# A four-layer network on one core: layer 0's attention as one chain over four quarters, layer 2's attention by rows as they are gathered

## The chip, the cores and the metric

The kernel runs on one core of one Trainium2 chip. The metric is the device time of one execution in microseconds (us), the median over several runs. A core has five engines that work side by side, each through its own queue in order: PE (TensorE, matrix products and transposes), DVE (VectorE), ACT (ScalarE), POOL (GpSimd) and SP (SyncE, which here only starts DMAs). POOL also starts the indirect DMAs, which gather or scatter single rows by a list of indices.

## The reference

Four layers of attention and feed-forward, with a layer norm behind each half, on x of 4 batches x 1024 tokens x 128 features, all float32:

```python
x = L0_attn_x
x = _layernorm(x + _L0_attn_ref(x, ...))   # convolution of 4 taps, cos/sin features, cumsum over time
x = _layernorm(x + _L0_ffn_ref(x, ...))    # x and weight rounded to an fp6 grid in blocks of 32, one product
x = _layernorm(x + _L1_attn_ref(x, ...))   # linear recurrence over time with a complex diagonal
x = _layernorm(x + _L1_ffn_ref(x, ...))    # 16 experts, the best 4 of each token, and a shared one
x = _layernorm(x + _L2_attn_ref(x, ...))   # causal softmax attention, 16 heads of 8 features, rotary
x = _layernorm(x + _L2_ffn_ref(x, ...))    # 8 experts, the best 2 of each token
x = _layernorm(x + _L3_attn_ref(x, ...))   # gated Toeplitz mixing
x = _layernorm(x + _L3_ffn_ref(x, ...))    # 32 experts, the best 4 of each token, and a shared one
return x
```

Layer 0's attention and layer 1's recurrence run along time, so a later part of the sequence needs the state of the earlier one, and layer 2 is causal. A router decides per token which experts it goes to.

## The kernel before

**Tiles.** The 4 x 1024 tokens are 32 tiles of 128. A quarter is 256 time steps of all four batches, 8 tiles; a half is two quarters. `tile_of` says which tile holds which piece of a batch. `x` holds the tokens with a token per partition, `xT` the same with a feature per partition.

**Generators.** Every stage is a Python generator that emits instructions and yields what they are thought to cost, a number in the manner of us. `run` emits one to its end. `mix(main, side)` emits a step of `main` and then as much of `side` as makes up its cost, times `pace`; each instruction of the side is put behind the latest of the main one on its engine (`queued`). With `drain=False` the rest of the side is left for later. `chain` puts generators one behind the other, `abreast` emits several in step, `press` emits a side until a condition holds. The order inside an engine's queue is then made from this order and from what each instruction waits for, so instructions without such a tie can stand earlier than they were emitted.

**Experts.** A router (`l1_route`) finds each token's experts and the position of each of its rows in a list that is sorted by expert (`positions`). `spread` scatters the tokens' rows into that list in DRAM, one indirect DMA of 128 rows for each tile and choice (64 for a half in layer 1). `small_experts` loads the list in groups of 512 rows, applies the experts' weights and stores the results; `collect` gathers them back, again 128 rows a DMA, and adds them, weighted, on DVE (L1359).

**The order before, up to layer 2.** Layer 0's attention of quarters 0 and 1 (`l0_attn((0, 1))`) with nothing beside it. The set-ups of layers 1 and 2. Layer 0's FFN and layer 1's recurrence of these two quarters, the latter beside the building of layer 2's expert weights (`l2_weights`). The first half's router. Layer 0's attention of quarters 2 and 3, its products on DVE instead of POOL (`no_pool`), beside the 64 scatters of the first half. The first half's experts, beside FFN and recurrence of quarters 2 and 3 (`beside=True`: in the side's PSUM). The shared expert with what is left of that side, beside `l1_close`, which collects the first half by quarters, normalizes and transposes it. Layer 2's attention of the first half, beside router and scatters of the second half. The second half's experts, layer 2's experts of the first half, layer 2's attention of the second half (`l2_attn(1)`) beside layer 2's results and layer 3's attention of the first half, and so on to the end of layer 3.

**PSUM.** The pool `side` has two buffers of one bank with the tag "s". Layer 0's attention holds one of them for `ms` through a whole quarter, from its first product (`headd` with `den`) to the square root `rs`, and takes the other for `z2` and `po`. The recurrence (`l1_attn`) keeps two, `pu[0]` and `pu[1]`, at the same time, since both are read for the real and for the imaginary part.

**Names.** In `l0_attn`: `t`, `k` (L432-L435) the phase and its rounding, `im`, `re` (L437, L440) sine and cosine, `times` (L442) their product with `pq`, `s` the cumulative sum (L358). In `l0_ffn`: `qt`, `xd` the rounding (four passes on POOL a quarter: L485, L495, L497, L525). In `l1_attn`: `b` (L641), `g` (L645). `norm` has three ways to the inverse root: ACT's square root, POOL's power, and Newton steps on DVE (`by="dve"`); its last step is L205. In `l2_attn`: `project` and `masks` make `qT` and `qm`, `scores` the products `sc` on PE, `weights` the exponential `pr` on ACT (L1049) and the mask multiplication on DVE (L1055), `values_of` the product with the values on PE (L157).

## Time and profile before

| What | us |
|---|---|
| Median of 11 runs (2535.01 to 2555.37) | 2545.76 |
| The profiled execution | 2543.54 |
| Its span, first to last instruction | 2541.6 |
| PE busy in it | 1697.8 (67%) |
| DVE busy | 1348.7 (53%) |
| ACT busy | 811.3 (32%) |
| POOL busy | 782.6 (31%) |
| First scatter of the first half (`l1ra`) starts | 311.87 |
| First rows of the experts' list load (`xg`) | 432.02 |
| First projection of layer 2's first half | 655.06 |
| PE clock granted, mean | 0.823 of full speed |

The profile gives, for one execution, the busy time of each engine (per stretch of time, if asked), the groups of instructions by line of the program with their mean durations and with what ended the engine's waits before them, and the chain that ended last: from the last instruction back, at each step to what released it. "Another core or an unknown queue" in that chain is a wait whose end the profile can't put down to an instruction; "issue" is time in which the engine waited for nothing that the profile shows. An operation is written as output<-inputs, by the program's names.

### The profile page before, as it was taken

How to read it: one execution, taken by the hardware profiler on the slowest of the kernel's cores; microseconds unless marked ns; L12 is line 12 of the kernel's file. 1: busy time of each engine (PE TensorE's matmuls, PEld its weight loads, DVE VectorE, ACT ScalarE, POOL GpSimd, SP SyncE). 2: the span in 40 equal slices, each digit the busy share in tenths (PEclk: the TensorE clock that was granted, in tenths of full speed). 3: DMA queues.
4: the chain of work that ended last, by engine and by line, in shares of the span. 5: the costliest groups of instructions: out<-in, count | busy, mean ns of one | idle time of the engine just before them, and what ended most of it. 6: DMA issues, size and time to landing. Idle time of an engine off the chain costs nothing.

```text
span 2541.6 us, 28615 instructions
## 1 busy us (share of the span) xinstructions
PE 1697.8 (67%) x9605; PEld 1030.7 (41%) x9605; DVE 1348.7 (53%) x3797; ACT 811.3 (32%) x1158; POOL 782.6 (31%) x725
## 2 busy tenths in 40 slices
PE   7538676873651875788897888868619896764810
PEld 3225333752320454555532332345416683642710
DVE  8864795856560672234546674735403565630453
ACT  5512362320320442222365545512102352320310
POOL 5432185235145004233220001020560203154364
PEclk9768787986775997898899988978859997876865
DMA  9902002341001143222300000030410331321422
GB/s 318 289 15 87 15 35 101 105 132 43 20 27 40 52 147 103 77 63 58 111 22 1 1 5 13 14 125 25 176 56 17 106 106 43 92 84 53 117 77 53
DMA packets 224007, 192.05 MB, mean 76 GB/s; under 512 B 16816, under 2 KB 204080, under 8 KB 222832
## 3 DMA queue, kind: packets, MB, share of 16 engines
q1 hardware_dynamic: 203152, 147.28, 18.4%
q0 software_dynamic: 20704, 42.86, 5.5%
q8 instruction: 83, 1.36, 0.2%
q14 instruction: 68, 0.56, 0.1%
HBM read 93.47 MB, written 96.60 MB: 75 GB/s over the span
## 4 chain that ended last, share of the span: by engine, by line
PE 41%; DVE 21%; another core or an unknown queue 14%; POOL 9%; issue 8%; ACT 3%; DMA 3%; SPq 0%; DVEq 0%; POOLq 0%; ACTq 0%
PE gu L157 11%; PE s L157 10%; PE sc L157 5%; PE yp L157 5%; PE tp L165 5%; POOL l1ra L1293 4%; POOL yt L1293 2%; DVE x L1359 1%; PE pu L157 1%; DVE pr L1055 1%; PE pg L157 1%; POOL l3rb L1293 1%; PE py L157 1%; DVE x L205 1%
## 5 line engine op out<-in xcount | busy, mean ns | idle before, releaser
L1049 ACT ACTIVATE pr<-sc 128x1024 f32<-128x1024 f32 x288 | 279.6, 1021 | 318.2 <-PE sc L157 217.5
L157 PE MATMUL gu<-ld,xgT 128*128 x768 | 204.1, 409 | 55.0 <-ACT xgT L167 21.5
L157 PE MATMUL sc<-qm,kT 32*128 32x512 f32 (+3 forms) x1536 | 199.4, 558 | 9.8 <-ACT pr L1049 6.2
L157 PE MATMUL s<-pr,va 128*32 128x512 f32 (+3 forms) x1536 | 178.0, 533 | 41.7 <-issue 23.8
L157 PE MATMUL gu<-wall,xgT 128*128 x352 | 182.4, 645 | 20.0 <-DMA wall<-wall 18.0
L157 PEld LDWEIGHTS gu<-ld,xgT 128*128 128x128 f32 x768 | 146.2, 201 | 86.8 <-ACT xgT L167 32.8
L165 PE MATMUL tp<-ld,hg 128*128 128x128 f32 x736 | 119.2, 284 | 92.0 <-ACT hT L167 38.3
L169 DVE COPY hT<-tp 128x512 f32<-128x512 f32 x140 | 95.7, 684 | 130.3 <-PE tp L165 71.9
L165 PEld LDWEIGHTS tp<-ld,hg 128*128 128x128 f32 x736 | 94.9, 147 | 151.5 <-issue 55.9
L1462 ACT ACTIVATE sg<-gu 128x512 f32<-128x512 f32 x88 | 52.4, 598 | 289.3 <-PE gu L157 182.2
L1689 DVE TENSOR_TENSOR hg<-sg,gu 128x256 f32<-128x256 f32 x192 | 78.4, 415 | 124.8 <-ACT sg L1688 112.4
L1055 DVE TENSOR_TENSOR pr<-pr,ld 128x512 f32<-128x512 f32 (+1 forms) x160 | 92.3, 580 | 96.9 <-ACT pr L1049 88.1
L157 PEld LDWEIGHTS sc<-qm,kT 32*128 32x128 f32 x1536 | 85.3, 197 | 114.9 <-issue 71.4
L1688 ACT ACTIVATE sg<-gu 128x256 f32<-128x256 f32 x192 | 73.0, 385 | 167.4 <-PE gu L157 109.7
L1464 DVE TENSOR_TENSOR hg<-sg,gu 128x512 f32<-128x512 f32 x88 | 60.0, 681 | 121.2 <-ACT sg L1462 78.2
L165 PE MATMUL tp<-ld,xg 128*128 128x128 f32 x472 | 78.3, 291 | 64.9 <-ACT hT L167 20.5
L167 ACT COPY xgT<-tp 128x512 f32<-128x512 f32 x118 | 69.2, 586 | 159.0 <-PE tp L165 130.0
L1293 POOL DMA_INDIRECT l1ra<-x,posl1a x64 | 95.6, 1494 | 60.7 <-DVE posl1a L1270 41.5
L1293 POOL DMA_INDIRECT yt<-l1yr,posl1r x64 | 60.8, 950 | 151.5 <-DVE x L1359 76.5
L157 PE MATMUL yp<-ld,hT 128*128 x768 | 103.9, 277 | 0.7 <-DVE hT L169 0.3
L157 PEld LDWEIGHTS s<-pr,va 128*32 128x32 f32 x1536 | 38.5, 113 | 151.9 <-issue 105.6
L157 PE MATMUL yp<-wall,hT 128*128 x704 | 98.5, 286 | 1.5 <-DVE hT L169 1.5
(433 smaller groups left out, 3527.7 us busy)
## 6 DMA issues: line engine op xcount, KB each, us to landing
wall<-wall SPq DMA_DIRECT2D x16, 768.0 KB
l3ra<-zero SPq DMA_DIRECT2D x1, 6144.0 KB
wall<-we SPq DMA_DIRECT2D x24, 256.0 KB
ld<-in_l_w SPq DMA_DIRECT2D x2, 3072.0 KB
ld<-in_l_w SPq DMA_DIRECT2D x1, 6144.0 KB
xg<-l3ra SPq DMA_DIRECT2D x24, 256.0 KB
l3ya<-yg SPq DMA_DIRECT2D x24, 256.0 KB
l1ra<-zero SPq DMA_DIRECT2D x1, 5120.0 KB
```

What stands on the lines that cost most here:

```text
L157: return self.nc.tensor.matmul(out, lhsT, rhs, start=start, stop=stop)
L165: nc.tensor.transpose(pt[:, k * P : (k + 1) * P], s, self.ident)
L167: nc.scalar.copy(dst, pt[:, : n * P])
L169: nc.vector.tensor_copy(dst, pt[:, : n * P])
L205: nc.vector.tensor_scalar(x, x, mv[:, t, 0:1], rstd[:, t : t + 1], ALU.subtract, ALU.mult)
L1049: nc.scalar.activation(pr, sc[h], AF.Exp)
L1055: nc.vector.tensor_tensor(d, d, cst["tril"].unsqueeze(1).unsqueeze(1).to_broadcast([P, 2, n, P]), ALU.mult)
L1293: ins = self.nc.gpsimd.indirect_dma_start(**kw)
L1462: nc.scalar.activation(sg, gu[:, 0, :], AF.Silu)
L1464: nc.vector.tensor_tensor(h, sg, gu[:, 1, :], ALU.mult)
L1688: nc.scalar.activation(sg, pg[:, :, 0, :], AF.Silu)
L1689: nc.vector.tensor_tensor(h[:, 2 * c : 2 * c + 2, :], sg, pg[:, :, 1, :], ALU.mult)
```

## The change

Layer 0's attention is one generator over all four quarters, the main one of one `mix`. Its side is, for each quarter as soon as its attention is listed (`after`), the FFN and the recurrence, and between quarters 1 and 2 the first half's router, then scatters and layer 2's weights abreast. The side is emitted with `pace=0.45`, and what is left of it goes on beside the shared expert and the experts of the first half, which now come in this order. `l1_close` goes by batches instead of quarters and is the side of layer 2's first half, together with the second half's router and scatters; `l2_attn` presses its side until a batch's row is listed before it prepares that batch, and counts its steps as 3.8 (first half) or 3.0 (second) instead of 2.3. The second half's `l1_wall` is loaded behind layer 2's first half. `norm` can do its last step on ACT (`on_act`). Some buffers change: `den`, `b` and `g` one each, `t` and `k` three, `im` and `re` in their place.

```diff
@@ Kernel.__init__
-        self.both = (self.first, Part("r", 2, 2))
+        self.both = (Part("a", 0, 2, range(B)), Part("r", 2, 2, range(B)))
@@ norm
+        if on_act:
+            off = self.tile(self.small, [P, n], f"off{n}")
+            nc.vector.scalar_tensor_tensor(off, mv[:, :, 0], -1.0, rstd, ALU.mult, ALU.mult)
         for t, x in enumerate(tiles):
-            nc.vector.tensor_scalar(x, x, mv[:, t, 0:1], rstd[:, t : t + 1], ALU.subtract, ALU.mult)
+            if on_act:
+                nc.scalar.activation(x, x, AF.Identity, bias=off[:, t : t + 1], scale=rstd[:, t : t + 1])
+            else:
+                nc.vector.tensor_scalar(x, x, mv[:, t, 0:1], rstd[:, t : t + 1], ALU.subtract, ALU.mult)
@@ l0_attn
-        times = nc.vector.tensor_tensor if no_pool else nc.gpsimd.tensor_tensor
+        times = lambda q: nc.vector.tensor_tensor if q in no_pool else nc.gpsimd.tensor_tensor
...
-                den = self.tile(bp, [P, QC], "den")
+                den = self.tile(bp, [P, QC], "den", bufs=1)
...
-                    t = self.tile(tp, [P, QC], "t")
+                    t = self.tile(tp, [P, QC], "t", bufs=3)
...
-                    k = self.tile(tp, [P, QC], "k")
+                    k = self.tile(tp, [P, QC], "k", bufs=3)
...
-                    im = self.tile(tp, [P, QC], "im")
+                    im, re = t, k
...
-                self.norm(self.quarter(q), by="act" if no_pool else "pool")
+                self.norm(self.quarter(q), by="act" if q in no_pool else "pool", on_act=True)
+                self.listed.add(f"l0 {q}")
@@ l0_ffn
-            qp = self.pool(ctx, "l0fq", 2, right=beside)
-            ps = self.side if beside else self.pool(ctx, "l0fps", 2, space=PSUM)
+            qp = self.pool(ctx, f"l0fq{qs[0]}", 1, right=True)
+            ps = self.side
...
-                self.norm(self.quarter(q), by="dve" if beside else "act")
+                self.norm(self.quarter(q), by="dve", on_act=True)
@@ l1_attn
-            tp = self.pool(ctx, "l1t", 2, right=beside)
-            ps = self.side if beside else self.pool(ctx, "l1ps", 2, space=PSUM)
+            tp = self.pool(ctx, f"l1t{qs[0]}", 1, right=True)
+            ps = self.side
...
-                (tt if beside else nc.gpsimd.tensor_tensor)(rows(g[0]), rows(g[0]), steps(pw[:, 0, :]), ALU.mult)
+                tt(rows(g[0]), rows(g[0]), steps(pw[:, 0, :]), ALU.mult)
...
-                self.norm(self.quarter(q), by="dve" if beside else "act")
+                self.norm(self.quarter(q), by="dve", on_act=True)
@@ l1_close
-        for q in range(part.q0, part.q0 + part.nq):
-            yield from self.collect("l1", part, K1, yp, (q - part.q0) * QT, QT)
-            self.norm(self.quarter(q))
...
+        for b in range(B):
+            yield from self.collect("l1", part, K1, yp, b * 4, 4)
+            tiles = part.order[b * 4 : b * 4 + 4]
+            self.norm([x[:, t, :] for t in tiles], by="dve")
+            for t in tiles[::2]:
+                nc.sync.dma_start(out=self.xsave[:, t : t + 2, :], in_=x[:, t : t + 2, :])
...
+            nc.vector.tensor_copy(xTv[:, b, 2 * hf : 2 * hf + 2, :], pt.rearrange("p (q t) -> p q t", q=2))
+            self.listed.add(f"row {hf}{b}")
@@ l2_attn, prepare(b)
+                self.press(side, lambda: f"row {hf}{b}" in self.listed)
@@ l2_attn, main loop
-                    took += 2.3
+                    took += 3.0 if hf else 3.8
@@ l2_weights
-                    nc.gpsimd.tensor_scalar(am, ab[:, i, :], self.cst["em"][:, e : e + 1], 2.0, ALU.mult, ALU.mult)
+                    nc.scalar.activation(am, ab[:, i, :], AF.Copy, scale=em[:, e : e + 1])
@@ new
+    def after(self, q):
+        yield from self.when(lambda: f"l0 {q}" in self.listed)
+        if q == 0:
+            self.l1_setup()
+            yield (20.0,)
+            self.l2_setup()
+            self.zero_lists("l1")
+            yield (4.0,)
@@ all
-                self.run(self.l0_attn((0, 1)))
-                self.l1_setup()
-                self.l2_setup()
-                weights = self.l2_weights()
-                next(weights)
-                self.zero_lists("l1")
-                self.run(self.l0_ffn((0, 1)))
-                self.run(self.mix(self.l1_attn((0, 1)), weights))
-
-                self.run(self.l1_route(a))
-                self.run(self.mix(self.l0_attn((2, 3), True), self.spread("l1", a, K1)))
+                main = self.l0_attn(range(NQT), (2, 3))
+                then = lambda q: self.chain(self.after(q), self.l0_ffn((q,)), self.l1_attn((q,)))
+                side = self.chain(
+                    then(0), then(1), self.l1_route(a1), self.abreast(self.spread("l1", a1, K1), self.l2_weights()),
+                    then(2), then(3),
+                )
+                self.run(self.mix(main, side, pace=0.45, drain=False))
                 self.zero_lists("l2", "l3")
                 with ExitStack() as c2:
                     wall = self.l1_wall(c2)
-                    yp = self.pool(c2, "l1ya", 5, right=True)
-                    side = self.chain(self.l0_ffn((2, 3), True), self.l1_attn((2, 3), True))
-                    self.run(self.mix(self.l1_experts(a, wall), side, drain=False))
-                    self.run(self.mix(self.chain(self.l1_shared(a), side), self.l1_close(a, yp)))
+                    self.press(side, lambda: "l1a" in self.listed)
+                    self.run(self.mix(self.chain(self.l1_shared(a1), self.l1_experts(a1, wall)), side))
+            with ExitStack() as c2:
+                yp = self.pool(c2, "l1ya", 5, right=True)
+                side = self.abreast(self.l1_close(a1, yp), self.chain(self.l1_route(r), self.spread("l1", r, K1)))
+                self.run(self.mix(self.l2_attn(0, side), side))
             with ExitStack() as c2:
                 wall = self.l1_wall(c2)
-                self.run(self.mix(self.l2_attn(0), self.chain(self.l1_route(r), self.spread("l1", r, K1))))
                 wall2 = self.l2_wall(c2)
...
-            self.run(self.mix(self.l2_attn(1), on, drain=False))
+            self.run(self.mix(self.l2_attn(1, on), on, drain=False))
```

## The prediction

> **What bounds the kernel now.** I read the stretches between the program's stages first (busy time of each engine), then the chain that ended last, then the timelines of the software DMA (POOL's gathers and scatters) and of PE beside them.
>
> Stretches (us, PE, PE load, DVE, ACT, POOL busy with instruction counts, PE clock, DMA share, GB/s): the first half's layers 0 and 1 up to its router; the second half's layer 0 attention beside the first half's scatter; the first half's experts; the rest up to layer 2; layer 2's first half.
>
> ```profile
> 154.00:310.00 156.00, 99.46 (x382) 60.59 (x386) 89.88 (x287) 35.20 (x54) 36.79 (x34) 0.77 0.11 41
> 310.00:432.00 122.00, 79.73 (x364) 37.36 (x356) 102.73 (x161) 61.52 (x70) 95.62 (x64) 0.79 0.16 61
> 432.00:540.00 108.00, 91.91 (x580) 78.63 (x580) 84.03 (x211) 38.36 (x79) 18.97 (x8) 0.96 0.34 98
> 540.00:660.00 120.00, 47.44 (x171) 29.34 (x172) 61.26 (x215) 12.54 (x20) 66.12 (x64) 0.63 0.26 81
> 655.00:927.00 272.00, 168.40 (x1297) 81.51 (x1295) 135.44 (x427) 86.18 (x91) 61.67 (x64) 0.78 0.09 35
> ```
>
> Two stretches have no busy engine. From 154 to 310 DVE works 58% of the time, and layer 0's other two quarters, which are mostly DVE work, wait behind it. From 540 to 660 PE works 47 of 120 us: POOL fetches the first half's 64 result rows, and layer 2 starts only when both quarters are collected. In 310 to 432 DVE is at 84%, and the 64 scatters last as long as the attention.
>
> The chain that ended last has 14% of the span under "another core or an unknown queue". Its largest piece lies in layer 2's first half; the lines after it are the stretches of that stall, of two runs of gathers in layer 2's second half, and of a clean piece of layer 2.
>
> ```profile
> 743.41 11.54 another core or an unknown queue
> 756.00 61.97 another core or an unknown queue
> ```
> ```profile
> 740.30:820.40 80.10, 13.46 (x56) 5.41 (x48) 4.84 (x13) 4.10 (x4) 52.27 (x55) 0.52 0.11 45
> 820.00:900.00 80.00, 69.55 (x587) 32.67 (x591) 51.23 (x133) 36.22 (x38) 0.00 (x0) 0.89 0.10 42
> 1261.20:1283.70 22.50, 17.67 (x98) 4.95 (x93) 6.10 (x11) 11.26 (x12) 8.27 (x9) 0.85 0.12 29
> 1312.00:1332.00 20.00, 18.61 (x152) 6.68 (x150) 10.82 (x40) 14.22 (x15) 6.66 (x6) 1.00 0.15 44
> ```
>
> While 64 scatters run back to back PE completes 56 matmuls in 80 us, against 587 in the next 80: about 75 us lost, 1.17 us a scatter. Twenty gathers beside layer 2 left 98 matmuls in 22.5 us where 164 would fit (9 us lost, 0.45 us each); twelve looser ones cost nothing. The first half's scatter shows no such stall. The cause isn't in the trace; I use the prices.
>
> **The sum** is made against the profiled execution, 2543.54 us (span 2541.6 and 1.9 outside); the median of the runs is 2.2 above it, which I add at the end.
>
> *1. The chain over four quarters, up to the first half's experts.* Before, scatters start at 311.87 and the first expert rows load at 432.0. After, the scatters need layer 0's FFN and layer 1's scan of quarters 0 and 1 and the router. The code decides how early: the side pool has two PSUM buffers; `ms` holds one for a whole main quarter, and `l1_attn` needs two at once (both `pu` are read for r = 0 and 1). So a quarter's scan can pass only between one `ms` and the next, and I expect the second scan when quarter 2 ends. DVE work up to then: 11 us idle at the start, 27 of setups (0-154 has 122 busy; two quarters take about 48 each), two POOL-helped quarters 96, one without POOL 53 (102.7 and some 8 ahead of 310, for two), two FFNs 33 (154-205 has 33.1), two scans 36 (205-285 has 35.9), part of quarter 3 18, three quarters of the router 15 (20.9 in 285-310): 289 us. DVE was 88% busy in 318-424 and 99.6% in 322-400; at 0.93, between the two, 11 + 278 / 0.93 gives 310, the start it has now (289 to 327 at the ends). So this edit brings **0** at this point; what it brings is that both attention quarters, and part of quarter 2's FFN, are behind us there. From there 64 scatters at 1.8 us (311.87 to 426.7) as now, or 1.265 if DVE leaves POOL alone. Bounds: start at 270 and 1.265 each, experts at 385 (-47); or see the third rival.
>
> The norm's last step goes to ACT: eight DVE instructions, 2.14 us a norm, for eight on ACT of about 0.28 (between 0.19 for 128x4 and 0.385 for 128x256, an estimate), 12 norms, 27 us on an engine 40% busy: hidden, and DVE's 26 us pay for the two Newton norms a quarter (some 2.5 us) and for L663 moved from POOL (1.2 instead of 3.3). `am` on ACT: 24 x 0.28, off POOL, where it would stand behind the scatters. `zero_lists` issues the same DMAs on SP, whose queue was full from 20 to 135 and idle to 220: nothing. One buffer less for `den`, `b` and `g` and the in-place `im`, `re`: nothing while the quarter's other tiles have three.
>
> The Trainium skill speaks against laying this scatter beside still more DVE work: "SBUF — State Buffer", section "SBUF: two separate sides", says that POOL's DMA descriptors can't be written while DVE holds the shared port in a two-port mode. This case's rows agree in direction: the 64 scatters beside the attention mean 1494 ns, the second half's gathers 950. By the lock alone, taken for every scatter, they would last longer than their 115 us; by the trace (DVE already 88% busy beside them in 318-424) they stay there, and I go by the trace.
>
> *2. From the experts to layer 2's first query.* Before 432 to 655: 223 us. After: `l1_shared` (542-583 with its waits, 22 clean) goes ahead of the experts, under the scatters' tail. Experts: 20 groups of 3.54 us (1002-1037) are 71 bare; beside FFN and scan of two quarters they took 108 (432-540). Some of quarter 2's side is done, but its four POOL passes (9.5 us a quarter) stand behind the scatters in POOL's queue, so I take 95. Then only batch 0's rows: 16 gathers of 1.25, 3 us landing, 16 adds of 0.34 partly under them, a norm, turn and copy of 7: 33 with PE idle. 128: **-95**. Bounds: 71 + 28 (-124) and 108 + 20 of a late scan + 33 (-62). The second half's router (20.9 of DVE) runs inside the 33, where DVE is free.
>
> *3. Layer 2's first half.* Before 272 us, 75 of them the stall. The same 64 scatters stay; 48 gathers (batches 1 to 3) come beside them, alternating on POOL. Bounds: 0 (the loose gathers) and 1.17 each, 56 us. The nearest row is that of gathers beside layer 2, 0.45: 22. On DVE 48 adds of 0.34, three norms, four copies stand in order ahead of the mask multiplications (L1055), which PE's value matmuls wait for; an add whose gather is late stops both. DVE is half busy: 8. **+30**, up to 60. `xsave` becomes 8 DMAs of 0.33 on SP: nothing.
>
> *4. The expert weights.* `l1_wall` moves behind layer 2's first half: 3 MB that were loaded under it now stand ahead of the second half's experts, on SP ahead of `l2_wall`'s eight. The nearest row is the wait for weights at 1659.81, 13.97 us; traffic reaches 2.75 MB in 10 us. **+12** (0 if memory is free early, 14).
>
> *5. Layer 2's second half* takes its side at 3.0 a step instead of 2.3, so layer 3's attention of the first half moves some 70 steps' cost from behind 1650 to before it, where PE is 82% busy. It can close part of the gap ahead of layer 3's scatter (1765-1790, PE 17 of 25), and lengthens 1248-1650. **0** (-15 to +12). The closing by rows in the second half has the same 64 gathers: nothing.
>
> Sum: 0 - 95 + 30 + 12 + 0 = -53: 2490.5, plus 2.2 for the median, 2492.7; as term 1's near bound (a start at 289 instead of 310) only lowers it, I say **2490**.
>
> **Rivals.** (a) *The side leads.* The scan of quarter 1 finds both PSUM buffers while quarter 2's `ms` isn't taken yet; scatters start near 270. For it: the pace of 0.45 puts the side early in program order. Against: `ms` of the next quarter is ready at once, the scan only after an FFN of 30 us. -53 - 45: 2446.
> (b) *POOL starves layer 2.* All 112 DMAs run dense, 1.17 each, and gathers wait behind scatters: 56 + 12 of DVE waits instead of 30: 2530. For it: a batch's 16 gathers and up to 26 scatters take 53 us, its attention 42. Against: no stall in the two looser rows.
> (c) *Slower: the side is shut out.* If no scan passes before the main chain ends, the chain takes DVE's 244 us (11 + 27 + 96 + 110) at 0.84, 290 us; then 156 us for FFN, scan and router as in 154-310, then 81 + 7 of scatters: experts at 534 instead of 432. 2493 + 102: 2595. It decides once experts start after 485. For it: the two buffers; PE's queue is in order, so a `pu` waiting for a buffer holds the main matmuls behind it. Against: at each quarter's end `ms` is free.
> (d) *The change does not do what it says:* layer 2 still waits for all rows. For it: `press` asks only at emission. Then 48 more gathers of 1.25 stand before it, 60 us instead of the 30 beside it: about 2520, inside the range.
>
> **How the numbers follow.** Forecast (with d) 0.46, its own range 2455 to 2525; (a) 0.18, 2400 to 2455; (b) 0.09; (c) 0.23, 2551 to 2620; nothing at all 0.04. The range leaves out the far end of (a) and the upper half of (c): 2420 to 2565. A measurement here tells 0.2%, 5 us, from no change: faster 0.73, same 0.04, slower 0.23.
>
> **What would show it.** Step 1: first `l1ra` scatter near 310, main attention done by then but for quarter 3; wrong if it starts after 360 or before 285. Step 2: first `qT` near 560, PE idle some 30 us before it. Step 3: layer 2's first half near 300 us, with "unknown queue" pieces over 80. Step 4: PE waiting for `ld<-in_l_w` some 12 us after it. Step 5: from the start of layer 2's second half to the end, within 15 us of now. The prediction is wrong if the gathers stall PE as scatters do, or if the scans stand outside the attention.

## The result, and the profile after

The changed kernel takes 2729.64 us (median of 8 runs, 2722.74 to 2736.34), the kernel before 2545.38 in the runs beside it (31 runs): a ratio of 1.0724, 95% interval [1.0709, 1.074]. That is 184 us slower where 55 us less were forecast; the range ended at 2565. Later runs on another chip gave 1.0724 [1.0676, 1.0772] again (after_again below). One run, the second of rows_only, fell in a slow state (3307 us, granted clock 0.57 against 0.81 in the first) and is left out everywhere.

The stretches of the changed kernel that answer to those of the prediction (us, then busy us and counts of PE, PE load, DVE, ACT, POOL, PE clock, DMA share, GB/s): up to the first scatter; the first half's scatters; from there to its experts; the experts; the rest up to layer 2's first scores; layer 2's first half.

```profile
175.00:389.00 214.00, 108.82 (x396) 60.01 (x395) 150.48 (x387) 74.89 (x110) 11.11 (x5) 0.69 0.00 0
389.00:470.00 81.00, 29.41 (x62) 13.03 (x62) 5.34 (x14) 8.96 (x21) 61.38 (x64) 0.58 0.27 102
470.00:629.00 159.00, 100.78 (x400) 60.33 (x400) 78.58 (x197) 47.99 (x96) 20.01 (x9) 0.73 0.13 48
629.00:715.00 86.00, 81.52 (x533) 73.89 (x533) 50.34 (x114) 36.02 (x79) 0.00 (x0) 0.96 0.42 120
715.00:787.00 72.00, 16.22 (x71) 9.55 (x69) 43.79 (x220) 3.70 (x5) 39.89 (x41) 0.57 0.20 58
787.00:1060.00 273.00, 144.27 (x1164) 68.08 (x1168) 124.47 (x363) 76.30 (x79) 84.61 (x87) 0.72 0.10 37
```

The second line is the one to stay with. Beside the scatters DVE, which was to be the bound up to the experts, works 5 of 81 us; before, it worked 103 of 122. POOL alone is busy, and PE does 62 matmuls.

For all kernels I take the same six points of the trace: the start of the first scatter of the first half's rows, of the first load of its expert rows (`xg`), of the first exponential of layer 2's first half, of the first load of the second half's expert rows, of the first exponential of layer 2's second half, and of the first load of layer 3's expert rows. The columns are the first two points, then the time from each to the next, then the rest and the span (us, of the profiled executions).

| Kernel | first scatter | experts' rows | to layer 2 | first half | to second half | to layer 3's rows | rest | span |
|---|---|---|---|---|---|---|---|---|
| before | 312 | 432 | 235 | 249 | 346 | 729 | 551 | 2542 |
| after | 389 | 629 | 158 | 273 | 379 | 746 | 545 | 2730 |
| own_psum | 376 | 496 | 214 | 267 | 388 | 745 | 547 | 2657 |
| weights_last | 391 | 586 | 197 | 268 | 384 | 753 | 546 | 2734 |
| own_wlast | 378 | 460 | 249 | 276 | 383 | 751 | 547 | 2666 |
| own_abreast | 377 | 471 | 232 | 270 | 378 | 744 | 552 | 2648 |
| chain_mended | 376 | 470 | 235 | 278 | 344 | 728 | 548 | 2604 |
| fills | (251) | 603 | 159 | 275 | 381 | 749 | 543 | 2710 |
| fills_late | (389) | 577 | 157 | 272 | 376 | 742 | 540 | 2664 |
| rows_only | 314 | 435 | 225 | 284 | 379 | 751 | 546 | 2620 |
| rows_oldclose | 315 | 436 | 225 | 284 | 358 | 747 | 543 | 2593 |
| rows_took | 315 | 436 | 225 | 284 | 358 | 729 | 550 | 2582 |
| early_rows | 315 | 434 | 205 | 283 | 347 | 737 | 549 | 2556 |
| paced | 314 | 432 | 236 | 211 | 337 | 732 | 547 | 2495 |
| paced_fast2 | 312 | 432 | 234 | 187 | 341 | 730 | 551 | 2474 |
| early_rows_paced2 | 315 | 434 | 203 | 240 | 350 | 729 | 553 | 2509 |
| after_paced * | 388 | 593 | 138 | 202 | 287 | 628 | 453 | 2301 |
| paced_fast * | 316 | 434 | 220 | 177 | 272 | 603 | 470 | 2175 |
| early_rows_paced * | 317 | 434 | 198 | 196 | 270 | 600 | 471 | 2170 |

(* on another kind of chip, where the kernel before takes 2168 us; see the last experiments. In brackets: the fills that stand for the scatters.)

Before to after: +197 up to the experts, -77 to layer 2, +24 in its first half, +34 to its second half, +17 to layer 3's rows, -6 behind them: 189, and 188 by the spans. The loss sits in the first number; some of it is won back on the way to layer 2, whose first scores come 120 us later than before (787 against 667).

Where it comes from is seen on DVE. Its timeline in the changed kernel (start, us, engine, line, operation, tiles, in brackets the idle time ahead and who ended it), three lines:

```profile
482.50 0.69 DVE L475 TENSOR_TENSOR x<-s,x 128x512 f32<-128x512 f32 x1 [87.75 <-PE s L157]
...
508.40 2.29 DVE L365 TENSOR_TENSOR_SCAN s<-keep,k 128x1024 f32<-128x1024 f32 x1 [16.41 <-ACT sq L453]
...
523.77 1.74 DVE L465 RECIPROCAL rs<-rs 128x256 f32<-128x256 f32 x1
```

L475 adds quarter 2's output projection (`po`) to `x`. Its factor `rs` was ready at 302, the projection comes at 481. From the end of `rs` to this add the four quarters take 15, 6, 11 and 8 us before, and 12, 67, 181 and 56 after (in own_psum, where the attention has buffers of its own: 14, 11, 15, 19). In the program's order of the tag "s", the first recurrence stands ahead of quarter 1's `po`; ahead of quarter 2's stand the second recurrence, the router's tiles (ready at 389) and 13 of the 24 tiles of layer 2's expert weights; ahead of quarter 3's `ms` stand 22 of them. PE works them off in the same order, 13 up to 481 and 22 up to 506. Its timeline between shows that these tiles are slow as well:

```profile
401.22 2.05 PE L157 MATMUL s<-ld,ld 128*128 128x512 f32 x2 [14.32 <-DMA ld<-in_l_big]
...
414.49 1.02 PE L157 MATMUL s<-ld,am 128*128 128x512 f32 x2
422.91 2.08 PE L157 MATMUL s<-ld,ld 128*128 128x512 f32 x2 [7.40 <-issue]
...
429.69 1.91 PE L157 MATMUL s<-am,ld 128*128 128x128 f32 x8
437.61 2.07 PE L157 MATMUL s<-ld,ld 128*128 128x512 f32 x2 [6.01 <-issue]
439.47 1.91 PE L157 MATMUL s<-ld,am 128*128 128x512 f32 x2
464.91 2.08 PE L157 MATMUL s<-ld,ld 128*128 128x512 f32 x2 [23.52 <-issue]
...
506.17 0.64 PE L157 MATMUL s<-den,ld 128*32 128x256 f32 x8
```

PE works steadily from 401 to 415, then in short bursts until the scatters end (469); from 475 on it runs freely again. The last line is quarter 3's `ms`, 204 us behind the end of quarter 2's `rs`. The profile puts PE's waits down to "issue", that is to nothing it shows, but ACT's timeline has something that stands ahead of them, the copies that empty the weight tiles (`we`):

```profile
422.27 0.59 ACT L1424 COPY we<-s 128x512 f32<-128x512 f32 x1 [9.26 <-issue]
...
436.97 0.59 ACT L1424 COPY we<-s 128x512 f32<-128x512 f32 x1 [8.90 <-issue]
...
464.27 0.59 ACT L1424 COPY we<-s 128x512 f32<-128x512 f32 x1 [26.42 <-issue]
```

Each burst of PE begins 0.05 us after such a copy ends, that is when a buffer of the ring comes free. The copy at 464.27 is the ninth; its product, the ninth tile (the line at 429.69), was complete at 431.6. So in this stretch ACT stands still with its input ready, and PE mostly waits for ACT.

The chain that ended last in layer 2's first half, and behind it (start, us, what):

```profile
790.68 38.91 issue
...
836.29 21.28 another core or an unknown queue
...
865.38 24.39 another core or an unknown queue
...
1069.65 11.67 DMA ld<-in_l_w
```

The stall of before (75 us beside 64 scatters) is there again, in three pieces, and the fourth line is the late load of layer 1's weights. In the kernel before, too, it isn't PE alone that stood still; here is DVE in the stall that the prediction reads, and PE behind it:

```profile
817.99 0.69 DVE L169 COPY t<-s 128x512 f32<-128x512 f32 x1 [62.00 <-remote]
818.74 1.87 PE L157 MATMUL s<-ld,t 128*128 128x8 f32 x8 [31.22 <-DVE t L169]
```

("remote" is the timeline's word for another core or an unknown queue.)

### The profile page after: what moved, and what is told of

Same layout as the page of the kernel before. It is cut to its first block, busy times and chain, and to the rows that moved or that the text cites. A ratio compares the mean times of both kernels' runs of the same rounds, so it can differ in the third digit from the quotient of the medians.

```text
span 2729.7 us, 28792 instructions
## 1 busy us (share of the span) xinstructions
PE 1733.9 (64%) x9605; PEld 1046.5 (38%) x9605; DVE 1374.1 (50%) x3896; ACT 841.3 (31%) x1256; POOL 727.0 (27%) x699
## 4 chain that ended last, share of the span: by engine, by line
PE 42%; DVE 24%; another core or an unknown queue 14%; issue 9%; ACT 4%; POOL 3%; DMA 3%; SPq 0%; DVEq 0%; POOLq 0%; ACTq 0%
PE gu L157 11%; PE s L157 11%; PE yp L157 5%; PE sc L157 4%; PE tp L165 4%; DVE s L365 2%; POOL yt L1306 2%; PE s L165 1%; DVE x L1372 1%; PE pg L157 1%; ACT pr L1062 1%; DVE bn L192 1%; DVE pr L1068 1%; PE py L157 1%
## 5 line engine op out<-in xcount | busy, mean ns | idle before, releaser
L157 PE MATMUL sc<-qm,kT 32*128 32x512 f32 (+3 forms) x1536 | 207.8, 584 | 46.9 <-issue 31.4
L157 PE MATMUL s<-pr,va 128*32 128x512 f32 (+3 forms) x1536 | 167.6, 536 | 20.7 <-DVE pr L1068 9.1
L1306 POOL DMA_INDIRECT yt<-l1ya,posl1a x64 | 61.9, 967 | 166.9 <-DVE g L779 115.4
L1306 POOL DMA_INDIRECT l1ra<-x,posl1a x64 | 61.8, 965 | 139.5 <-DVE posl1a L1283 120.3
```

Source lines behind the costliest of these rows:

```text
L157: return self.nc.tensor.matmul(out, lhsT, rhs, start=start, stop=stop)
L1306: ins = self.nc.gpsimd.indirect_dma_start(**kw)
```

## The experiments

### The side buffers and the order of the side

own_psum:

```diff
-            psz = self.pool(ctx, "l0z", 2, space=PSUM)
+            psz = self.pool(ctx, "l0z", 1, space=PSUM)
...
-            pss = self.side
+            pss = self.pool(ctx, "l0m", 2, space=PSUM)
```

> The changed kernel, with one edit: the attention chain of layer 0 gets two PSUM buffers of its own for ms, z2 and the output projection (taken from z, which keeps one of its two). Theory 1 (buffers: ms and the projection of quarters 2 and 3 stand in the ring of two side buffers behind the scans, the router and the 24 tiles of layer 2's expert weights): the gap from 350 to 506 us closes, rs of quarters 2 and 3 come near 280 and 400 in place of 300 and 524, the experts start at 430 to 520 in place of 629, and the kernel takes 2530 to 2630. Rival (PE starved by the 64 scatters, whoever holds the buffers): PE works again about 39 of the 101 us beside the scatters, the experts start later than 580, and the kernel takes 2680 or more. Rival (one z buffer costs as much as it brings): quarters 0 and 1 end later than 100 and 175 us by over 15 us each.

2661.36 us, ratio 1.0466 [1.0434, 1.0498]; experts at 496 in place of 629, `rs` of the four quarters at 117, 194, 266 and 329. The attention is no longer halted, so the two shared buffers are shown as the main cause of the 197 us (133 of them). The whole time is 31 us above the theory's band: 56 of the 133 come back as a longer way to layer 2 (214 against 158), whose first scores come 77 us earlier (710 against 787). The lost `z` buffer costs quarter 0 15 and quarter 1 17 us, which the third theory had as its mark; it costs nothing at the end, as the attention is over 196 us earlier. What stays are 64 us by which the scatters start later than before, and this, in the stretch from the first scatter to the experts:

```profile
376.00:496.00 120.00, 66.92 (x199) 34.03 (x198) 10.30 (x22) 24.22 (x53) 61.87 (x64) 0.74 0.27 101
```

DVE works 10 of 120 us. The FFN of quarter 2 is emitted behind scatters and weights, and what stands in DVE's queue ahead of it is the shared expert's addition to `x` (L829), which has to wait until the scatters have read these rows, 60 us in two pieces, the longer one:

```profile
448.72 0.69 DVE L829 TENSOR_TENSOR x<-py,x 128x512 f32<-128x512 f32 x1 [39.79 <-DMA l1ra<-x,posl1a]
```

weights_last and own_wlast (the second with own_psum's edit):

```diff
-                    then(0), then(1), self.l1_route(a1), self.abreast(self.spread("l1", a1, K1), self.l2_weights()),
-                    then(2), then(3),
+                    then(0), then(1), self.l1_route(a1), self.spread("l1", a1, K1),
+                    then(2), then(3), self.l2_weights(),
```

> The changed kernel with the making of layer 2's expert weights (24 tiles through the side buffers) moved from beside the scatter to the end of the side chain, behind the scan of quarter 3. Theory 1 (buffers): quarter 2's projection follows the router directly, near 390 to 400 in place of 481, quarter 3's ms near 410 in place of 506; the experts start at 520 to 560 in place of 629; the 24 tiles then cost 20 to 60 us beside or behind the experts; in all 2640 to 2700. Rival (scatters starve PE whatever stands in its queue): PE still does under half of its work rate in the stretch with scatters, the experts start later than 590, and in all 2710 or more.

2736.33 us, 1.0761 [1.073, 1.0792]: experts at 586, 43 us earlier and short of the 69 to 109 expected, and 39 us of it come back as a longer way to layer 2, where the 24 tiles now stand. The theory's first marks came (quarter 2's projection at 390, quarter 3's `ms` at 391), but quarter 3's projection then follows its `rs` (412) only at 538: in the ring it stands behind FFN and recurrence of quarter 2, which end at 500 and 528. PE does 16 of 84 us beside the scatters, as the rival said, and the whole time is in the rival's band (2710 or more), though the experts start 4 us ahead of it. Taking only the weights out of the ring gains nothing.

> own_psum with the 24 tiles of layer 2's expert weights moved behind the scan of quarter 3 (both edits together). In own_psum the attention ends at 345 us and nothing but the weights stands beside the scatters (376 to 457), yet the experts start 39 us after them. If the stores of the weights on SP's queue and their tiles hold the experts back: experts start at 460 to 475 in place of 496, with the tiles' 20 to 50 us showing again up to layer 2; in all 2630 to 2660. If PE's starvation by the scatters is what holds everything: experts start at 490 or later.

2664.23 us, 1.0484 [1.0401, 1.0567]: experts at 460, as soon as the 64 scatters are through, as the first theory said; the way to layer 2 grows by 35, and layer 2's first scores come at 710 in both; the whole time is 4 us above the band. The weights cost the same in these two places.

own_abreast (own_psum with):

```diff
-                    then(0), then(1), self.l1_route(a1), self.abreast(self.spread("l1", a1, K1), self.l2_weights()),
-                    then(2), then(3),
+                    then(0), then(1), self.l1_route(a1),
+                    self.abreast(self.spread("l1", a1, K1), self.chain(then(2), then(3), self.l2_weights())),
```

> own_psum with the side put in another order: FFN and scan of quarters 2 and 3, then the weights, stand abreast of the 64 scatters in place of behind them. In own_psum and own_wlast the attention is over at 332 to 345 us and DVE works 10 of the 120 us from 376 to 496, because the FFN of quarter 2 is queued behind the scatters. If that queue is what keeps layer 2 late (first scores at 709): scans over by 480 to 520 in place of 540 to 620, experts at 465 to 490, first scores at 610 to 640, and 2560 to 2600 in all. Rival (scatters beside busy engines slow down and starve PE as much as is won): first scores at 680 or later, 2640 or more.

2650.26 us, 1.0422 [1.0392, 1.0452]; first scores at 703. My theory fell: the last multiplication of quarter 3's recurrence ends at 553, not 480 to 520. Beside the 64 scatters (377 to 468) PE does 98 matmuls in 91 us, but here that isn't the scatters' direct doing alone: DVE's L829 waits 45 us, in four pieces, for the scatters to have read `x`, with all that stands behind it in DVE's queue, and PE waits 32 us for L829. The order of the side can't be judged while that holds.

### Do the scatters starve PE?

In fills a POOL addition stands for each scatter; in fills_late it is a multiplication that reads `pos`, so that it can't run before the router (both leave out the first half's scatters). The edit of fills:

```diff
-                ins = self.indirect(
+                ins = self.fill() if lay + part.name == "l1a" else self.indirect(
...
+    def fill(self):
+        t = self.tile(self.small, [P, 4, D], "fill", mybir.dt.bfloat16, bufs=1)
+        z = self.zero.unsqueeze(1).to_broadcast([P, 4, D])
+        ins = self.nc.gpsimd.tensor_tensor(t, z, z, ALU.add)
...
+        return ins
```

> The changed kernel with the 64 scatters of the first half's rows into layer 1's lists left out; in the place of each stands one POOL addition over 128x512 that nobody reads, of 1.2 to 1.4 us, so that POOL's queue stays as full as before (the first half's experts then read zeroed rows). Theory 2 (the scatters themselves starve PE): PE does the 24 weight tiles in 45 to 60 us in place of 107, and quarter 3's ms and the end of the attention move forward by 45 to 60 us: experts start at 570 to 585 in place of 629. Rival (order of the side tiles and POOL's queue, not the scatters): the 24 tiles still take 95 us or more and the experts start at 615 to 640.

2711.44 us (one run): the 24 tiles take 53 us in place of 107 (first to last copy), as the theory said, but the experts start at 603, outside both bands. The fills didn't wait for the router and ran from 251 to 349, where they held up POOL's passes of quarter 1 (its recurrence ended 31 us later): two effects in one number.

> As fills, but the 64 POOL additions read the table of positions, so that they stand where the scatters stood (from 389 us on, behind the router) and POOL is as busy there as in the changed kernel; the scatters are left out again. In fills they ran from 251 us and held up POOL's passes of quarter 1. Theory 2 (scatters starve PE): the 24 weight tiles take 45 to 60 us in place of 107, experts start at 565 to 585 in place of 629, and PE does more than 45 us of work between 389 and 470 in place of 29. Rival (order and POOL's queue alone): tiles 90 us or more, experts at 615 to 640.

2666.15 us (one run), experts at 577: 52 us earlier. In the scatters' stretch:

```profile
389.00:470.00 81.00, 59.61 (x244) 30.18 (x244) 24.50 (x40) 32.69 (x65) 76.00 (x66) 0.84 0.27 100
```

With POOL even fuller than in the changed kernel (76 of 81 us against 61), but with no scatters, PE does 244 matmuls there in place of 62, and the 24 tiles take 52 us in place of 107. It is the DMAs that hold up the stretch, not POOL's queue, and they take 52 of the 197 us. fills and fills_late are single runs.

"Starve PE", my words in the expectations, is too narrow. ACT is held in this stretch (above), and DVE elsewhere. The same 32 instructions of the router (L704), first for the first half, with no gathers beside them, then in the changed kernel for the second half beside gathers (us of the window, busy us and count of DVE, PE clock, DMA share, GB/s):

```profile
378.00:382.00 4.00, 2.47 (x32) 0.50 0.01 2
738.00:761.00 23.00, 3.71 (x32) 0.50 0.17 44
```

From first to last they take 2.5 us in the first case (378.7 to 381.2) and 20.5 in the second (739.2 to 759.7), with waits of up to 1.3 us between them that the profile calls "issue". Where I say "starve" from here on, the other engines are meant, not PE alone.

### The gathered rows alone

rows_only is the kernel before with the parts of the diff in `l1_close`, `l2_attn`, `logits` and the two `Part`s, and with this in `all`:

```diff
-                    self.run(self.mix(self.chain(self.l1_shared(a), side), self.l1_close(a, yp)))
+                    self.run(self.chain(self.l1_shared(a1), side))
...
+            with ExitStack() as c2:
+                yp = self.pool(c2, "l1ya", 5, right=True)
+                side = self.abreast(self.l1_close(a1, yp), self.chain(self.l1_route(r), self.spread("l1", r, K1)))
+                self.run(self.mix(self.l2_attn(0, side), side))
```

As in the change, layer 1's weights for the second half are loaded behind this.

> The kernel before with the second part of the change alone: layer 1's rows of each half gathered, added and turned one batch row at a time, the first half's beside layer 2's attention, the second half's beside layer 2's experts; layer 0 and the scans stay as before. From the stretches of the changed kernel (72 less up to layer 2, 18 more in its first half, 12 for the weights, 58 more from there to the second half, 25 less behind): 2545 - 9 = 2536, with the first experts at 432 as before. By the prediction's terms 2 to 5: 2490. If the 58 us belong to layer 0's new order and not to the rows: 2478.

2621.54 us (one run), 78 above before. All my sums were too low. The gain up to layer 2 is 10 us, not 72: the rows are fetched only when the recurrences of quarters 2 and 3 are through (first gather at 587), and the first row then takes 72 us to the first scores. Part of these on the timelines of PE, ACT and DVE, and the stretch of the first gathers:

```profile
598.87 6.85 PE L157 MATMUL s<-ld,xT 128*128 128x16 f32 x32
626.93 0.38 ACT L757 ACTIVATE sc<-s 128x256 f32<-128x256 f32 x1 [25.94 <-remote]
627.35 0.43 DVE L759 TENSOR_TENSOR s<-sc,rows 128x256 f32<-128x256 f32 x1 [17.13 <-ACT sc L757]
```
```profile
587.00:627.00 40.00, 9.05 (x42) 8.30 (x40) 12.77 (x64) 2.52 (x4) 27.36 (x28) 0.53 0.18 47
```

The second half's router has 16 small products to do, and PE does them without a stop (the 32 matmuls of the first line, through at 605.7). It is ACT's sigmoid on them that comes 21 us later, held beside the gathers, and DVE's next router step waits for it. Row 0's norm stands in DVE's order among the router's steps.

rows_oldclose keeps the closing by quarters for the second half (the old `l1_close` under another name, `Part("r", 2, 2)` in its old order).

> As rows_only, but the second half's rows are closed by quarters as before (eight tiles at a time in a ring of five buffers, no draining after each batch row). If the closing by batch rows is what makes the stretch ahead of layer 2's second half 58 us longer: 40 to 60 us below rows_only, 2478 to 2496. If the stretch is longer for another reason: within 10 us of rows_only.

2599.22 us, 1.0222 [1.0174, 1.0269]: 21 us less in the stretch to the second half (379 to 358), 27 in all, so half of what I expected, but well off the rival's 10. The gathers' row among the groups (busy us, mean ns, idle time ahead and who ended it), first of rows_only, then of rows_oldclose:

```profile
L1299 POOL DMA_INDIRECT yt<-l1yr,posl1r x64 | 60.6, 947 | 171.6 <-DVE x L1365 102.9 <-DMA ld<-in_l_swu 50.4 <-issue 18.0
```
```profile
L1314 POOL DMA_INDIRECT yt<-l1yr,posl1r x64 | 60.7, 949 | 148.0 <-DVE x L1380 79.9 <-DMA ld<-in_l_swu 49.9 <-issue 17.9
```

The gathers cost the same; by batch rows they wait 23 us more for DVE's additions. That fits `collect`, which empties its ring of buffers at the end of every call, four in place of two.

rows_took is rows_oldclose with:

```diff
-                    took += 3.0 if hf else 3.8
+                    took += 2.3 if hf else 3.8
```

> rows_oldclose with the second half of layer 2 taking its side work at 2.3 a step as before in place of 3.0. Theory (the stretch from layer 2's second half to the rows of its next experts is 41 us longer because the side is taken faster): that stretch comes back from 412 to 371 us, the one behind it from 335 to 358; net 10 to 20 us less, 2575 to 2585. Rival (the stretch is longer for another reason, such as the earlier gathers of layer 2's own rows): 405 us or more in that stretch and the same time within 6 us.

2586.48 us, 1.0178 [1.0102, 1.0255]: from layer 2's second scores to its next rows 373 us in place of 412, from there to layer 3's rows 356 in place of 335; 18 less in that column, 13 by the medians (another chip of the same kind). The mechanism is as expected, the time 1.5 us above the band: the faster side moves work forward and loses a little by it.

early_rows: layers 0 and 1 as before, the second half as in rows_took, `l1_wall` ahead of layer 2's first half, and

```diff
+                    close = self.l1_close(a1, yp)
+                    self.run(self.mix(self.chain(self.l1_shared(a1), side), close, drain=False))
...
+                side = self.abreast(close, self.chain(self.l1_route(r), self.spread("l1", r, K1)))
+                self.run(self.mix(self.l2_attn(0, side), side))
```

> The order of before for layers 0 and 1; gathered rows in the first half alone, begun beside the second half's scans (as before) and going on beside layer 2's first half; layer 1's weights loaded ahead of that half as before; second half's rows by quarters and 2.3 a step as before. Theory (in rows_only nothing is won because the rows are fetched only when the scans of quarters 2 and 3 are through at 590 us, and 62 us pass from the first gather to the first scores): first scores near 615 to 630 in place of 667 before and 660 in rows_only, no wait for weights of 12 us, first half 35 us longer, the rest as before: 2525 to 2550. Rival (the scans of quarters 2 and 3 end as late whatever stands beside them, and the second half's router behind them): first scores at 650 or later and 2555 to 2580.

2551.46 us (8 runs), 1.0033 [1.0015, 1.0052], 1.5 above the theory's band. First scores at 640, between the two bands; the first half 34 us longer (283 against 249), the weights' 12 us gone. So the rows, at their best, win 27 us ahead of layer 2 and pay 34 in it.

chain_mended: own_abreast with the second half closed by quarters, 2.3 a step, and the weights loaded early.

> own_abreast with the three smaller costs taken back: the second half's rows closed by quarters (21 us), its side taken at 2.3 a step (11 to 18), layer 1's weights loaded ahead of layer 2's first half (12 to 13). By the sum of the terms 44 to 52 us less than own_abreast: with 2560 to 2600 there, 2510 to 2555 here, near or just below before. Rival: the terms overlap and under 30 us come back.

2606.41 us, 1.025 [1.022, 1.0279], 44 us less than own_abreast, the low end of the sum: the three terms add up. The level was wrong with own_abreast's.

### Scatters that wait for matmuls

paced is the kernel before with

```diff
                 done.append(ins)
+                if paced:
+                    self.tc.add_manual_dep(
+                        ins.ins, self.latest[mybir.EngineType.PE],
+                        mybir.DependencyInfo(mybir.DependencyClass.Sync, mybir.DependencyReason.DATA), reason="paced",
+                    )
+                    yield (1.26,)
...
-                self.run(self.mix(self.l2_attn(0), self.chain(self.l1_route(r), self.spread("l1", r, K1))))
+                self.run(self.mix(self.l2_attn(0), self.chain(self.l1_route(r), self.spread("l1", r, K1, True))))
```

> The kernel before with one edit: each of the second half's 64 scatters beside layer 2's first half waits for the matmul of layer 2 that stands ahead of it in program order, so that they are spread over the attention instead of running back to back. Theory (dense scatters starve PE: 56 matmuls in 80 us against 587 in the next 80; loose ones do not): the stall of some 75 us shrinks to under 25, layer 2's first half takes 185 to 215 us in place of 246, and the kernel 2490 to 2520. Rival (each scatter costs PE its 1.2 us wherever it stands): the first half stays within 10 us of 246. Rival (the last scatters come late and hold up the next experts): the half is shorter, but the gap to the next experts grows from 3 us to over 20.

2497.98 us, 0.9823 [0.9795, 0.9852]. Layer 2's first half takes 168 us to its last exponential in place of 246; 43 come back as late scatters, the third theory's mark. Both stretches:

```profile
740.00:836.00 96.00, 80.08 (x775) 39.56 (x771) 65.63 (x173) 48.19 (x50) 31.74 (x32) 0.97 0.14 57
836.00:879.00 43.00, 8.71 (x60) 6.01 (x56) 11.45 (x43) 0.27 (x1) 31.00 (x32) 0.64 0.50 197
```

Beside 32 scatters spread over 70 us (in groups, 2.2 us each on average) PE works 80 of 96 us. All 64, dense, had cost some 75 us.

paced_fast adds `pace=0.7` to that `mix`, early_rows_paced is early_rows with waiting scatters and gathers, after_paced the changed kernel with waiting scatters in both halves and waiting gathers of the first half's rows.

> The changed kernel with its software DMAs of layer 1's first half and of the second half's scatter made to wait: each of the 64 scatters beside layer 0's attention, of the 64 beside layer 2's first half and each gather of the first half's rows waits for the matmul of the main chain ahead of it in program order. Theory (dense software DMAs starve PE): layer 2's first half takes 170 to 210 us in place of 273 (plus a gap of up to 40 for late scatters); the experts start up to 50 us earlier than 629, as in fills_late, or, where the paced scatters wait for an attention that itself waits for the side buffers, not earlier; 2600 to 2680 in all. Rival (the half is long because of the rows' own work on DVE and POOL): 255 us or more in that half.

> paced, with the side of layer 2's first half taken at 0.7 of its cost, so that router and scatters come earlier in the program. In paced the first scatter starts at 766 and half of the 64 stand behind the attention (836 to 877, PE 9 of 43 us). Theory (late scatters only): the first starts near 735, the last lands within 10 us of the attention's end, the half takes 170 to 190 us, and the kernel 2460 to 2480. Rival (closer scatters starve PE again): the half takes 205 us or more, 2490 or more.

> early_rows (gathered rows in the first half alone) with the second half's 64 scatters and the rows' gathers waiting for matmuls as in paced. Theory (rows beside layer 2's first half cost 34 us there only because 112 dense software DMAs starve PE): first scores near 640 as in early_rows, half 180 to 215 us in place of 280, gap under 30, 2460 to 2500, so as good as paced_fast or better by up to 27. Rival (waiting gathers come late for their rows, and PE waits for the rows instead): half over 230 us, 2510 or more.

These three ran on a chip on which the kernel before takes 2167.72 us (19 runs, 2161.35 to 2175.06), so the expected times don't apply. Against it after_paced has 1.062 [1.0574, 1.0666], paced_fast 1.004 [1.0023, 1.0057], early_rows_paced 1.0022 [1.0005, 1.0039]. Up to the experts this chip is no faster (434 in both unchanged orders). Where software DMAs run dense, it is. The 32 scatters of layer 2's rows beside the second half's experts, the same instructions in the program, first early_rows on a chip of the first kind, then early_rows_paced on this one:

```profile
956.00:996.00 40.00, 12.03 (x46) 9.47 (x46) 5.04 (x15) 3.29 (x7) 30.17 (x32) 0.59 0.35 117
```
```profile
864.00:903.00 39.00, 36.31 (x220) 32.41 (x221) 18.39 (x42) 15.85 (x34) 29.30 (x31) 0.90 0.67 202
```

PE does 220 matmuls in place of 46. In these runs that chip doesn't show the starvation, and pacing brings nothing there. It separates the causes: in after_paced against paced_fast, which has the order of before up to layer 2, the experts still start 160 us later (593 and 434). The changed kernel without waiting scatters wasn't run there, so a part of the 160 can be theirs; they end 11 us later than in the changed kernel (480 against 469), and the experts start 113 behind them.

> The changed kernel as it is. On a chip where the kernel before takes 2168 us: by the stretches of after_paced against paced_fast on that chip (161 later experts, 82 won up to layer 2, some 34 in its first half, 50 behind it, 35 back at the end) 2280 to 2320, a ratio of 1.05 to 1.07: the order of the side buffers alone makes the change a loss, and the starvation only adds to it. If starvation were the main cause: 2230 or less there. On a chip where before takes 2543: 2725 to 2735 again.

> paced_fast again. On a chip where before takes 2543: first half 170 to 190 us and a gap under 15 to the next experts, 2455 to 2480 (in paced 2498). If the closer scatters starve PE again: 2490 or more. On a chip where before takes 2168: within 0.5% of before, as there was nothing to win.

> early_rows_paced again. On a chip where before takes 2543: first scores near 640, half 185 to 225 us, 2455 to 2495; if gathers cost PE as much as scatters even when paced, 2510 or more. On a chip where before takes 2168: within 0.5% of before.

These ran on a chip of the first kind (before 2545.51). after_again: 2725.81, 1.0724 [1.0676, 1.0772], stretches within 5 us of the first profile. paced_fast2: 2483.99 (4 runs), 0.9778 [0.9743, 0.9813], 0.16% above the band that I gave; first half 182 us and a gap of 4.5. It is the fastest version found there, on those chips. early_rows_paced2: 2499.29, 0.9827 [0.9791, 0.9863], in place of 2455 to 2495: its first half with gap is 240 us, 53 longer than paced_fast2's, more than the 31 won ahead of it. (These stretches are from its longest run, 2510.91, and paced_fast2's shortest, 2475.72; the medians are 15 us apart.) With waiting gathers too, this version of the rows doesn't pay. The stretch with layer 2's 32 scatters, now for the same kernel as on the other chip, has PE at 46 matmuls again, against 220 there:

```profile
911.00:951.00 40.00, 10.49 (x46) 8.41 (x46) 5.10 (x15) 3.30 (x7) 30.16 (x32) 0.63 0.35 117
```

## Why the prediction was wrong

**Term 1 (0) was the failed step; it measured +197.** I wrote that up to the experts DVE's work at 0.93 sets the pace, and used the two side buffers only to ask when the side's `pu` may pass. The ring binds the other way too: `po` and the next `ms` of the main chain come behind every tile that the side was given earlier. The step "what it brings is that both attention quarters ... are behind us there" is what the runs refute: at the first scatter (389) quarter 2's projection was 92 us off (481) and quarter 3's `ms` 117 (506). I had costed the 24 weight tiles only by ACT's 24 x 0.28, not as 24 places in the ring, 13 of them ahead of quarter 2's projection. By the runs: own buffers bring 133 of the 197 back (77 of the 120 by which layer 2 starts later); of the rest, 64, the later start of the scatters is the whole. There the sum itself was off: DVE had worked 310 us up to 376 in own_psum (its busy time in the stretches up to there), not 289, as quarter 3 was done by then, and 66 idle, not 21: 38 of these fall ahead of 154, where the kernel before, too, has 32. In the changed kernel 52 of the 197 are the scatters holding up the weight tiles (fills_late). These parts overlap, for own buffers also take the attention out from behind those tiles; on the chip without starvation 160 stay, with waiting scatters. The term's near bound was summed wrongly as well: a start at 270 and 64 scatters at 1.265 end at 351, and the experts would follow near 356, not 385.

**Rival (c)** named the ring but turned it round (the side shut out by the main chain) and priced it at 102, with 0.23. Its "decides once experts start after 485" came true.

**Term 2 (-95) measured -77.** The experts took 86 us in place of 95, the way from them to the scores 72 in place of 33. The 33 had PE idle anyway; what was missed is that the second half's router, put at nothing there because "DVE is free", stands in DVE's order ahead of row 0's norm and is held beside the gathers: 13 of the row's 16 additions are through at 739, the other three come at 760, the norm's last step at 772.5, and between the thirteenth and the fourteenth lie the 20.5 us of L704. And the gain is no gain of the rows: alone they bring 10. By the order of the stages it is work of quarters 2 and 3, done ahead of the experts, where the 197 stand.

**Term 3 (+30) measured +24**, and between +18 and +35 in the kernels whose scatters and gathers don't wait. The mechanism, a stall beside DMAs, was right. The size came right by luck: the price of 0.45 us a gather counts twenty gathers, but the line it is read from has nine POOL instructions (x9) in its 22.5 us, and the other eleven ran ahead of it; 9 us over nine are 1.0 each, and 48 of them with DVE's 8 us would have been 56.

**Term 4 (+12) was right**: 11.67 us in the chain, and with the weights loaded early that column is 12 us shorter (346.9 in early_rows, 358.5 in rows_took).

**Term 5 (0) measured +21 and +11.** That "the closing by rows in the second half has the same 64 gathers: nothing" forgot the ring of five: 21 us (rows_oldclose). The side at 3.0 a step is the 11 (17 less 6), within its bounds of -15 to 12; rows_took has it as 13 to 18.

**Rivals (a), (b) and (d)** didn't come: the scatters started later, not earlier; layer 2's first half shows no more than the known stall; and its first scores (787) came long before the last of the rows' gathers (929). The Trainium skill's rule ("SBUF — State Buffer", section "SBUF: two separate sides"), that POOL's descriptors can't be written while DVE holds the shared port in a two-port mode, agrees in direction with the rows: the 64 scatters of the first half took 965 ns each with DVE idle beside them, 1494 before with DVE at 84%. The rule was no help with the sign: the scatters were quicker in the changed kernel, and the other engines paid for it.

## What to carry to other kernels

Where two chains draw tiles from one small PSUM ring, write out the order of all its tiles, fillers too: each chain is as late as the last foreign tile ahead of it, and the engine that was the bound goes idle. Cost a dense run of software DMAs by what the other engines do beside it in the trace, not by POOL's time, and make the DMAs wait for matmuls before moving stages around them: one such edit brought 45 us here, and 62 with an earlier side (paced_fast2), about what the whole change was to bring; on the chip without starvation it brought nothing. Where the profile has "issue" ahead of PE, look at what empties its PSUM buffers. And where a part of a change is priced by a stall, ask first whether that stall can be removed by itself.

## What the hardware showed

- PE, ACT and DVE come nearly to a stop beside dense software DMAs (1.25 to 1.27 us apart): 62 matmuls in 81 us against 244 with POOL multiplications in their place, 46 in 40 us against 220 for the same kernel on the other chip; one ACT copy 26 us late with its input ready; 32 small DVE instructions in 20.5 us that take 2.5 elsewhere. The engines first go on for a while (to 415 in the changed kernel, where the scatters run from 389; to some 743 in layer 2 of the kernel before, where they run from 728). Spread to 2.2 us each on average, in groups, the DMAs cost nearly nothing (PE 80 of 96 us). The same section of the Trainium skill says that a DMA cannot be slowed by a compute operation, and the reverse; these runs show compute instructions delayed by DMAs, whatever the path (the profile has it as "issue" or an unknown queue, and no run here shows what the engines wait for).
- Whether it happens depends on the chip, as far as one such set of runs can tell. Five sets of runs were on chips on which the kernel before takes 2542 to 2546 us, one on a chip where it takes 2168, with the same times up to 434 us and the same granted clock up to there (0.81 in before and in paced_fast). What differs between the chips isn't in the traces.
